# One graph attention layer on one core: the node stage reordered, a fourth gather buffer, marks made in the loop, x loaded by GpSimd

## The chip, the core and the metric

The kernel runs on one core of one Trainium2 chip. The metric is device time of one execution in microseconds, median of several runs. The core has five instruction streams: TensorE (PE), VectorE (DVE), ScalarE (ACT), GpSimd (POOL) and SyncE (SP, which here only issues DMAs). Each runs its own instructions in program order and waits for the others by semaphores.

## The reference

12,500 nodes with 128 channels, 400,000 edges sorted by their destination, 32 edge attributes, 8 heads of 16.

```python
h = relu(layernorm(x))
message = (h @ w_src + b_src)[src] + (h @ w_dst)[dst]
rad = silu(silu(edge_attr_32 @ w1 + b1) @ w2 + b2) @ w3 + b3
message = (message * edge_weight1 * rad) @ w_sep + b_sep      # 8 heads x (16 alpha + 16 value)
score = einsum('ehk,ahk->eh', smooth_leaky_relu(alpha), alpha_dot)
att = segment_softmax(score, dst)
out = x + segment_sum(value * att, dst) @ w_proj + b_proj
```

## The kernel before

**Tables.** `x` stands in 98 tiles of 128 nodes, taken four at a time as Q = 25 quads. For each quad, `stats` (DVE, L237) and `scales` (ACT square root L242, DVE L243 and L244) give mean and scale, `norm` (ACT L253, POOL L256, two tiles each) normalises, `turn` (PE L265, DVE L267) transposes and applies the ReLU, and `products(i, 0)` multiplies by w_src and `products(i, 1)` by w_dst (PE L276, ACT copy L282, SP stores L290 and L292 to the DRAM tables t_src and t_dst). The loop over i runs them ahead of each other by fixed distances. From i = 10 on, each round makes a product of both tables, the targets ten quads behind. Beside these stand the loads of weights and constants (`weights_list`, SP), and the order check: `falls` compares each destination with the next (DVE L309), `fits` counts the violations (PE L321 and L323, DVE to L326) into the number `bad`. `spans`, `cuts` and `places` prepare small tables; the end of `cuts` (L403 to L408) writes a DRAM row `same` which tells, edge by edge, whether a segment begins.

**Branch.** All engines then load `bad` (L1517). At zero the sorted-by-destination path `windows()` runs, the only one that these inputs take; `Else` is a general path that does not run.

**Main loop.** The edges form 782 sections of 512 (`SEC`), two to a step: `step(k)` for k = -5 to 390 (NP = 391 steps), software-pipelined by hand. For a step k:
- `gather(k, f)` (POOL L877, two calls a step, four gathers of 128 rows each): an indirect DMA brings rows t_src[src] into a tile `gs`. It goes out in step k - 2. `gs` has three buffers for each f, so a gather waits till the tile of step k - 3 was read.
- `load_w` (SP L849) brings 1024 edge weights to all partitions as w_b, three buffers; `load_d`, `load_md` (d_b, md), `load_e` (ACT L825, edge attributes e_t) the rest.
- `e_T`, `mlp1` to `mlp3` and `radial` (L887 to L936) make the radial weights, `sources` (PE L944) transposes the gathered rows, `one_hot_T` and md (L951) add the target rows, `message` (DVE L958) forms the message mT.
- `alphas` (PE L964, ACT L966, DVE L971) and `scores` (PE L980, ACT L992 or L997) make scores Sp, which SP stores to DRAM and reads back as S (L995, or L998 and L1003) in blocks of MP = 8 steps. A block's softmax follows: the flags sm of `load_sm` (L1006), spread over the partitions by PE (L1013), the running maxima (DVE L1018, L1023), the subtraction (L1032), the exponential Pr (ACT L1028) and its transposes (PE L1047, ACT L1050 and L1057).
- Twelve steps later (LAG), `values` (PE L1077, DVE L1079), `one_hot` and `sums` (PE L1090, DVE L1094) add values into a window of 64 nodes, ob, which is stored twice: to the accumulator agg (L1114) and, by `store_win` (L1098), to a table of window rows.

The zeroing of agg (L140, L142, SP) also runs in the first steps.

**Tail.** After the last gathers come steps NP to NP + 12, with the jobs listed at L1414 for the rows on window borders: `block_rows` (rr, L1164), `last_rows`, `block_totals` and two scatters comb into agg (POOL L1228, behind 11 others). Between these steps ACT loads x back, as x_fin (L1450, L1452). `final` divides, projects and adds x.

**What sets the order.** It is written out by hand: each engine's stream is the order in which `step` and the node stage's loop call the functions. A tile name with `bufs=n` turns over n buffers, and a new writer waits for the readers of the tile n turns back.

Of the kernel before, what the change touches and what calls it, by code (L numbers as in the profile page):

```python
# [30 lines left out]
P = 128  # L31
# [25 lines left out]
def gnn_kernel(ctx: ExitStack, tc: tile.TileContext, a: dict, out: bass.AP):  # L57
# [9 lines left out]
    NX = -(-NP // MP) * MP * PR  # L67
# [17 lines left out]
    same = dram.tile([1, NX + 1], BF16, name="same")  # L85
# [44 lines left out]
    nc.vector.scalar_tensor_tensor(spread, below, float(H), above, op0=ALU.is_lt, op1=ALU.mult)  # L130
    zc = 5
# [26 lines left out]
    with tc.tile_pool(name="node", bufs=2) as np_, tc.tile_pool(name="node1", bufs=1) as n1, \  # L158
# [32 lines left out]

        def load_targets():
# [16 lines left out]
        def weights_list():  # L209

            pairs = []
            for name, t in wt.items():
                ap = a[name]
# [13 lines left out]
            return [lambda t=t, ap=ap: nc.sync.dma_start(out=t, in_=ap) for t, ap in pairs]  # L227
# [31 lines left out]
        def turn(i):  # L259
# [3 lines left out]
            for t in range(t0, t1):  # L263
# [3 lines left out]
            nc.vector.tensor_scalar(x_all[:, t0:t1, :].rearrange("p u n -> p (u n)")[:, :w],  # L267
                                    pt.rearrange("p u n -> p (u n)")[:, :w], 0.0, None, op0=ALU.max)

        def products(i, k):  # L270
# [6 lines left out]
            u = 4 * (i % 2) if k else 0  # L277
            if u == 0:
                mds[k] = np_.tile([P, 4 + 4 * k, C], F32, name=f"ms{k}", bufs=4 if k else 6)
# [3 lines left out]
            if k and i % 2 == 0 and i + 1 < Q:  # L283
# [27 lines left out]
        def fits():  # L311
# [14 lines left out]
            nc.vector.tensor_copy(bad, sum_)  # L326
            nc.sync.dma_start(out=ends_d[:, 1:2 * NS + 1].rearrange("o (p c) -> (o p) c", p=NH),
# [8 lines left out]
            places_load()  # L336
# [15 lines left out]

        def places():

            on = n1.tile([NC, P], F32, name="on")
            nc.vector.tensor_tensor(on, to[:, 0, :], to[:, 1, :], op=ALU.is_equal)
            nc.vector.scalar_tensor_tensor(on, on, SKIP, to[:, 0, :], op0=ALU.mult, op1=ALU.add)
# [28 lines left out]
        def cuts():  # L386

            pv = nps.tile([P, 4, P], F32, name="pt")
            nc.tensor.matmul(pv[:, 0, :], bvb, w_proj, start=True, stop=True)
            nc.vector.tensor_add(b_out, pv[:, 0, :], b_out)  # L390
            nc.tensor.transpose(pv[:, 1, :], bvb, ident)
            nc.vector.tensor_scalar(bare[:, 0:C], pv[:, 1, :], -1e-16, None, op0=ALU.mult)
            nc.vector.tensor_copy(z.rearrange("p (t c) -> p t c", c=ROW),
                                  bare[:RP].unsqueeze(1).to_broadcast([RP, zc, ROW]))
# [1192 lines left out]
```

## Time and profile before

| what | us |
|---|---|
| median of 3 runs | 4141.16 (4141.04 to 4141.25) |
| profiled execution | 4142.2 |
| span from its first to its last instruction | 4140.4 |
| first gather starts | 77.37 |
| last gather ends | 4008.67 |
| POOL: gathers of L877 | 3125, busy 2971.4 |

The busy shares are of the span. In the group rows, a line holds the engine, the operation, the tiles by the program's names, the count, busy time and mean nanoseconds; behind the second bar stands the idle time of the engine just ahead, and what ended most of it. In rows in order of time, the start and the length come first, and the bracket gives the idle time ahead and what ended it; "issue" means that nothing was waited for. "SPq", "ACTq" and "POOLq" are issues of DMAs.

### The profile page before, as it was taken

The page shows a single profiled execution, that of the slowest core. Times are in us where ns is not written, and L with a number is a line of the kernel's source. Part 1 is how long each engine was busy: PE and PEld are TensorE (multiplying, and loading weights), DVE is VectorE, ACT ScalarE, POOL GpSimd, SP SyncE. Part 2 cuts the span into 40 slices and gives each one's busy share as a digit, 9 for nine tenths or more (in the row PEclk, how much of TensorE's full clock was granted, in tenths as well). Part 3 has the DMA queues.
Part 4 walks back from the last instruction along what each step waited for, and adds up shares of the span by engine and source line. Part 5 has one row for each costly group of instructions (what it writes and reads, how often), then busy time and mean ns, then how long its engine had stood idle before and what let it go on. Part 6 is the DMA issues. An engine that isn't in the chain of part 4 may idle for free. (4 is left out here: it accounts for less than half of the span.)

```text
span 4140.4 us, 87674 instructions
## 1 busy us (share of the span) xinstructions
PE 3922.6 (95%) x29351; PEld 2370.2 (57%) x29351; DVE 3079.2 (74%) x6182; ACT 1895.2 (46%) x4549; POOL 3031.8 (73%) x3218
## 2 busy tenths in 40 slices
PE   7789999999999999999999999999999999999997
PEld 6355555655555555555555555555555555555556
DVE  5567777777777778777777777777777777777775
ACT  5344444444444444444444444444444444444442
POOL 4777777777777777777777777777777777777762
PEclk8899999999999999999999999999999999999998
DMA  7767777767777777777777776767767767777754
GB/s 264 226 168 195 194 181 199 199 180 191 201 187 182 196 190 181 193 198 190 180 194 196 178 197 181 188 172 191 188 171 192 188 180 179 190 184 172 193 157 179
DMA packets 593219, 782.99 MB, mean 189 GB/s; under 512 B 125441, under 2 KB 392062, under 8 KB 592628
## 3 DMA queue, kind: packets, MB, share of 16 engines
q1 hardware_dynamic: 384520, 513.29, 42.8%
q0 software_dynamic: 100416, 205.44, 23.4%
q10 hardware_dynamic: 107820, 58.56, 5.0%
q8 instruction: 234, 3.83, 0.4%
q14 instruction: 229, 1.88, 0.1%
HBM read 637.82 MB, written 139.23 MB: 188 GB/s over the span
## 5 line engine op out<-in xcount | busy, mean ns | idle before, releaser
L877 POOL DMA_INDIRECT gs<-t_src,idx x3125 | 2971.4, 951 | 975.8 <-issue 792.2
L966 ACT ACTIVATE sl<-pa,c_b_a 128x512 f32<-128x512 f32 x782 | 536.9, 687 | 1117.4 <-PE pa L964 1106.3
L971 DVE SCALAR_TENSOR_TENSOR al<-pa,sl 128x512 f32<-128x512 f32 x782 | 539.4, 690 | 518.1 <-ACT sl L966 508.8
L1077 PEld LDWEIGHTS V<-c_w_v,mT 128*128 128x128 f32 x6064 | 737.7, 192 | 298.0 <-DVE ob L1094 156.0
L1077 PE MATMUL V<-c_w_v,mT 128*128 128x128 f32 x6064 | 867.7, 286 | 0.0
L964 PE MATMUL pa<-mT,c_w_a 128*128 128x512 f32 x1564 | 804.6, 596 | 3.8 <-DVE mT L958 2.5
L1079 DVE TENSOR_TENSOR pvx<-V,Pem 128x512 f32<-128x512 f32 x758 | 519.3, 685 | 236.9 <-PE V L1077 222.3
L944 PEld LDWEIGHTS pm<-ident,gs 128*128 128x128 f32 x3125 | 395.5, 141 | 516.4 <-issue 392.2
L936 DVE SCALAR_TENSOR_TENSOR rad<-p,c_fc_b,w_b 128x512 f32<-128x512 f32 x782 | 550.0, 745 | 121.6 <-PE p L928 90.4
L944 PE MATMUL pm<-ident,gs 128*128 128x128 f32 x3125 | 497.7, 276 | 75.1 <-DMA gs<-t_src,idx 73.8
L958 DVE SCALAR_TENSOR_TENSOR mT<-pm,c_b_src,rad 128x512 f32<-128x512 f32 x782 | 550.1, 745 | 5.2 <-PE pm L951 4.8
L1090 PEld LDWEIGHTS misc<-pvx,oh 128*64 128x64 f32 x6250 | 353.1, 138 | 316.2 <-ACT h L900 303.4
L914 ACT ACTIVATE h<-p,b 128x512 f32<-128x512 f32 x391 | 287.9, 736 | 405.4 <-PE p L911 317.9
L1090 PE MATMUL misc<-pvx,oh 128*64 128x136 f32 x6250 | 453.5, 287 | 19.8 <-ACT h L900 13.6
L928 PE MATMUL p<-h,w3b 64*128 64x512 f32 x1564 | 409.0, 600 | 7.7 <-ACT h L914 7.4
L951 PE MATMUL pm<-ohT,m 64*128 64x512 bf16 x2346 | 322.4, 380 | 0.0
L896 PE MATMUL m<-eT,w1b 64*128 64x256 f32 x782 | 277.3, 435 | 1.0 <-ACT eT L889 1.0
L896 PE MATMUL misc<-eT,w1b 64*128 64x256 f32 x782 | 277.3, 435 | 0.0
L997 ACT ACTIVATE Sp<-m,b_s 128x512 f32<-128x512 f32 x192 | 131.7, 686 | 301.0 <-PE m L980 299.0
L911 PE MATMUL p<-h,w2b 64*64 64x256 f32 x3128 | 260.6, 404 | 2.1 <-DVE rad L936 2.1
L900 ACT ACTIVATE h<-misc,b 128x256 f32<-128x256 f32 x391 | 192.8, 493 | 150.1 <-PE misc L896 148.4
L1063 DVE TENSOR_TENSOR oh<-lane,misc 128x504 f32<-128x504 f32 x391 | 261.3, 668 | 0.0
(174 smaller groups left out, 3685.4 us busy)
## 6 DMA issues: line engine op xcount, KB each, us to landing
w_b<-in_edge_weight SPq DMA_DIRECT2D x390, 512.0 KB
d_b<-in_dst SPq DMA_DIRECT2D x390, 256.0 KB
gs<-t_src,idx POOLq DMA_INDIRECT x3125
e_t<-in_edge_attr ACTq DMA_DIRECT2D x390, 128.0 KB
sc_d<-Sp SPq DMA_DIRECT2D x192, 256.0 KB
win<-ob SPq DMA_DIRECT2D x390, 68.0 KB
agg<-ob SPq DMA_DIRECT2D x782, 33.5 KB
md<-t_dst SPq DMA_DIRECT2D x782, 32.0 KB
```

The source lines that it names most:

```text
L877: nc.gpsimd.indirect_dma_start(out=gs[:, t, :], out_offset=None, in_=t_src[:, :], in_offset=bass.IndirectOffsetOnAxis(ap=idx[:, t0 + t:t0 ...
L896: nc.tensor.matmul(p1[q], w1b[s, :], eTs[k][s, :], start=True, stop=True)
L928: nc.tensor.matmul(p3s[k][:, f, 0:SEC], w3b[s, :], h2s[k][s, :], start=True, stop=True)
L936: nc.vector.scalar_tensor_tensor(rad[:, s], p3[:, f, 0:n], b3, w_g[k][:, s], op0=ALU.add, op1=ALU.mult)
L944: nc.tensor.matmul(pms[k, f][:, t * T:(t + 1) * T], gs[:, t, :], ident, start=(t == 0), stop=False, is_transpose=True, skip_group_check=True)
L958: nc.vector.scalar_tensor_tensor(mTs[k][:, s], pms.pop((k, f))[:, 0:n], b_n, rad[:, s], op0=ALU.add, op1=ALU.mult)
L964: nc.tensor.matmul(pa[:, 0:n], w_a, mTs[k][:, f * SEC:f * SEC + n], start=True, stop=True)
L966: nc.scalar.activation(sl[:, 0:n], pa[:, 0:n], AF.Silu, bias=b_a, scale=1.0)
L971: nc.vector.scalar_tensor_tensor(al, pa, 0.25, sl, op0=ALU.mult, op1=ALU.add)
L1077: nc.tensor.matmul(V[:, t, :], mTs[c][:, o:o + T], w_v, start=True, stop=True)
L1079: nc.vector.tensor_mul(pvx[c][:, f, 0:n, 0:C].rearrange("p t (h k) -> p t h k", h=H), V[:, 0:n, :].rearrange("p t (h k) -> p t h k", h=H), ...
L1090: nc.tensor.matmul(acc[f * W:(f + 1) * W, :], ohs[c][:, f * TS + t, :], pvx[c][:, f, t, :], start=(t == 0), stop=(t == n - 1), skip_group_ ...
```

## The change

In the node stage all 25 source products come ahead of the target products. The statistics run two quads further ahead, `h` has six buffers, ACT normalises one tile of a quad and POOL three, ACT applies the ReLU of odd quads, and the rows of t_src are stored two quads at a time. `falls` follow target products 0 to 3, and `count`, the part of `fits` that makes `bad`, target product 6. The smaller preparations move behind them. Five weights that only `Else` reads are loaded there, the other loads alternate between SP and ACT, and ACT runs one Silu ahead of the branch.

In the loop, `gs` has four buffers, `w_b` two and `ob` three; `load_w` goes out one step ahead rather than two, and d_b and w_b of step 0 ahead of the loop. `same` is no longer written: `load_sm` loads the destinations of a block and `marks` compares them on DVE two steps later, 49 times.

In the tail POOL loads x_fin behind its 11 scatters, and ACT stores the last rows rr straight from ob, step by step, where SP stored windows and read them back.

```diff
@@ norm, turn, products
-            hs[i] = np_.tile([P, 4, C], F32, name="h", bufs=4)
+            hs[i] = np_.tile([P, 4, C], F32, name="h", bufs=6)
...
-                if t - t0 < 4 - 2:
+                if t == t0:
...
+            if i % 2:
+                nc.scalar.activation(x_w, p_w, AF.Relu)
+            else:
+                nc.vector.tensor_scalar(x_w, p_w, 0.0, None, op0=ALU.max)
...
-                mds[k] = np_.tile([P, 4 + 4 * k, C], F32, name=f"ms{k}", bufs=4 if k else 6)
+                mds[k] = np_.tile([P, 8, C], F32, name=f"ms{k}", bufs=4)
@@ cuts: the flags
-            nc.scalar.dma_start(out=same[:, 0:E].rearrange("o (p c) -> (o p) c", p=P), in_=sm)
...
-            nc.scalar.dma_start(out=same[:, E:NX + 1], in_=more)
@@ loop of the node stage
-            if i >= 10:
-                products(i - 10, 1)
+            if i >= 25:
+                products(i - 25, 1)
             products(i, 0)
-            if i + 5 < Q:
-                stats(*quads[i + 5])
-            if i % 2 and i + 4 < Q:
-                scales(quads[i + 4][0], quads[min(i + 5, Q - 1)][1])
+            for j in range(i + 7 if i else 5, min(i + 8, Q)):
+                stats(*quads[j])
+            if i == 0:
+                scales(quads[5][0], quads[6][1])
+            if i % 2 and i + 6 < Q:
+                scales(quads[i + 6][0], quads[min(i + 7, Q - 1)][1])
...
             if i >= 3:
-                for load in (next(more, None), next(more, None)):
+                for eng in (nc.sync, nc.scalar):
+                    load = next(more, None)
                     if load:
-                        load()
-            if 8 <= i < 12:
-                falls(i - 8)
+                        load(eng)
             if i == 13:
                 fits()
-        for i in range(Q - 10, Q):
+        places_load()
+        for i in range(Q - 25, Q):
             products(i, 1)
-            if i == Q - 6:
+            if i < 4:
+                falls(i)
+            elif i == 6:
+                count()
+            if i == Q - 10:
                 spans()
-        cuts()
+                places_make()
+            elif i == Q - 6:
+                cuts()
+            elif i == Q - 4:
+                score_bias()
+            elif i == Q - 3:
+                places()
+        warm = n1.tile([1, 1], F32, name="warm")
+        nc.scalar.activation(warm, eps[0:1, :], AF.Silu)
@@ the loop's tiles
-                w_g[k] = lp.tile([P, PR], F32, name="w_b", bufs=3)
+                w_g[k] = lp.tile([P, PR], F32, name="w_b", bufs=2)
...
-                gs = lp.tile([P, TS, C], F32, name=f"gs{f}", bufs=3)
+                gs = lp.tile([P, TS, C], F32, name=f"gs{f}", bufs=4)
...
-                ob = sp.tile([P, ROW], F32, name="ob", bufs=5)
+                ob = sp.tile([P, ROW], F32, name="ob", bufs=3)
@@ load_sm and the new marks
-                at = same[0:1, m * MQ * SEC:m * MQ * SEC + 1]
-                nc.sync.dma_start(out=sms[m], in_=bass.AP(at.tensor, at.offset, [[SEC, MQ], [1, SEC + 1]]))
+                t = dms[m] = sp.tile([MQ, SEC + 2], I32, name="dm", bufs=1)
...
+                nc.sync.dma_start(out=t[q0:q1, :], in_=bass.AP(
+                    at.tensor, at.offset + e0 + q0 * SEC, [[SEC, q1 - q0], [1, SEC + 2]]))
+
+            def marks(m):
+                t = dms.pop(m)
+                sms[m] = sp.tile([MQ, SEC + 1], BF16, name="sm")
+                nc.vector.tensor_tensor(sms[m], t[:, 0:SEC + 1], t[:, 1:SEC + 2], op=ALU.not_equal)
@@ step
-                if has(k + 2):
-                    load_w(k + 2)
+                if has(k + 1) and k > -1:
+                    load_w(k + 1)
...
-                        if k == NP + LAG:
-                            last_rows_2()
+                        if c - 1 >= last * SB:
+                            last_rows(c - 1)
...
+                if has(k - 2) and (k - 2) % MP == 4:
+                    marks((k - 2) // MP)
@@ tail
-            x_loads = load_xb(x_fin)
+            load_xb(x_fin, nc.gpsimd)
...
+            def last_rows(c):
+                q, s = width(last) // 2, 2 * (c - last * SB)
...
                 for i in range(2):
+                    nc.scalar.dma_start(out=rrs[last][i * q + s:i * q + s + 2, :],
+                                        in_=accs[c][i * (W - 1):i * (W - 1) + W + 1:W, :])
...
-                for _ in range(3):
-                    next(x_loads, None)
```

What stands in the engines' streams, first on PE at the end of the node stage. `pt<-ident,h` are transposes of `turn`, `pm<-w_nodes,x_all` the products (four matmuls to a quad, source and target alike), `tot` the sums of the order check. Before:

```order
L265 MATMUL pt<-ident,h 128x128 x4
L276 MATMUL pm<-w_nodes,x_all 128x128 x8
L265 MATMUL pt<-ident,h 128x128
L265 MATMUL pt<-ident,h 128x84
L276 MATMUL pm<-w_nodes,x_all 128x128 x13
L276 MATMUL pm<-w_nodes,x_all 84x128
L276 MATMUL pm<-w_nodes,x_all 128x128 x37
L276 MATMUL pm<-w_nodes,x_all 84x128
```

After, from the same place on:

```order
L269 MATMUL pt<-ident,h 128x128
L269 MATMUL pt<-ident,h 128x84
L283 MATMUL pm<-w_nodes,x_all 128x128 x5
L283 MATMUL pm<-w_nodes,x_all 84x128
L283 MATMUL pm<-w_nodes,x_all 128x128 x28
L328 LDWEIGHTS ones_b
L328 MATMUL tot<-gt,ones_b 1x512
```

Before, each round held eight product matmuls, and ten target quads followed the last source quad (84x128 is its last tile). After, the sources end before any target; seven target quads (28 matmuls) stand between them and the check's sums, and 18 quads behind.

Second, ACT behind the last scores (Sp). Before:

```order
L992 ACTIVATE Sp<-m_51451,b_s 64x128
L992 ACTIVATE Sp<-m_51451,b_s 32x384
L1450 DMA x_fin<-xb 128x1792 x3
L1057 COPY pvx<-Pem 128x4x8 x2
L1450 DMA x_fin<-xb 128x1792 x3
L1057 COPY pvx<-Pem 128x4x8 x2
L1450 DMA x_fin<-xb 128x1664
L1452 DMA x_fin<-xb 84x128
L1057 COPY pvx<-Pem 128x4x8 x2
L1028 ACT_TABLE_LOAD
L1028 ACTIVATE Pr<-M 128x512
```

After:

```order
L1011 ACTIVATE Sp<-m_51522,b_s 64x128
L1011 ACTIVATE Sp<-m_51522,b_s 32x384
L1092 COPY pvx<-Pem 128x4x8 x6
L1063 ACT_TABLE_LOAD
L1063 ACTIVATE Pr<-M 128x512
L1085 COPY Pem<-misc 128x256 x2
```

The eight loads of x_fin are gone from between the copies. They are on POOL, whose stream after the change reads there:

```order
L896 DMA gs_51217<-t_src,idx 128x128
L1263 DMA agg<-e_t,ids 12500x136 x11
L1481 DMA x_fin<-xb 128x1792 x6
L1481 DMA x_fin<-xb 128x1664
L1482 DMA x_fin<-xb 84x128
L1263 DMA agg<-comb,ids 12500x136 x2
```

They stand between the 11 early scatters and the two of comb.

More of the change, by code (lines that the diff above doesn't have):

```diff
@@ L776, in windows @@
             prep, e_g, d_g, w_g, md, gath = {}, {}, {}, {}, {}, {}
[L777 to L778 removed]
+            eTs, h1s, h2s, ohT, m3, mr, mTs, als, S_all, sms, Ps, Pem, pvx, ohs, accs, xs, Ms, pms, p3s, rads, rel, locs, made, dms = (
+                {} for _ in range(24))
             def prep_load(u):
@@ L1520, in gnn_kernel @@
     with fit.Else():
+        for name in spare:
+            nc.sync.dma_start(out=wt[name], in_=a[name])
         for i in range(NZ):
```

79 lines of the change are left out of this document (37 added, 42 removed).

## Prediction, made before the changed kernel ran

> **What bounds the kernel now.** I read the page's busy shares and costliest groups first, then busy time by stretches, then the order of time of each engine at the start, at the one long stall, and behind the last gather. The profiled execution took 4142.2 us around a span of 4140.4; the runs' median is 4141.16. I work every term out in the span and take the sum off the median, 1.0 us below the profiled execution.
>
> ```profile
> span 4140.4 us, 87674 instructions
> PE 3922.6 (95%) x29351; PEld 2370.2 (57%) x29351; DVE 3079.2 (74%) x6182; ACT 1895.2 (46%) x4549; POOL 3031.8 (73%) x3218
> L877 POOL DMA_INDIRECT gs<-t_src,idx x3125 | 2971.4, 951 | 975.8 <-issue 792.2
> 2000.00:2200.00 200.00, 193.91 (x1459) 115.39 (x1458) 152.36 (x308) 91.23 (x220) 151.49 (x160) 1.00 0.74 194
> ```
>
> The shares mislead: PE shows 95% and POOL 73%, but POOL's gap between gathers is mostly "issue", which means that it waited for nothing. In 200 us it issues 160 gathers, 1.25 us each (0.95 busy, 0.30 issue), and never more. PE is busy 193.9 of the same 200 us. So POOL paces the middle and PE follows 3% behind its limit. The gathers form one chain from the first to the last:
>
> ```profile
> 77.37 1.19 POOL L877 DMA_INDIRECT gs<-t_src,idx  x1 [15.91 <-DMA t_dst<-ms]
> 225.54 0.94 POOL L877 DMA_INDIRECT gs<-t_src,idx  x1 [7.07 <-PE pm L944]
> 4007.73 0.94 POOL L877 DMA_INDIRECT gs<-t_src,idx  x1 [0.30 <-PE pm L944]
> ```
>
> The span is 77.4 us ahead of the first gather, 3931.3 from it to the end of the last (4008.67), and 131.7 behind it. Inside the chain is one long stop, 7.07 us, 6.8 more than the usual 0.30. The number of gathers and their work stay, so the change can gain ahead of the chain, at that stop, and behind the chain.
>
> **Head: the node stage.** Ahead of 77.37 POOL idles 15.9 us for node rows. The program's waits say for which: all t_src stores (the row's name, t_dst, is the nearest landing), and `bad`, which was made long before.
>
> ```profile
> 46.40 0.14 DVE L326 CAST bad<-sum__607 1x1 int32<-1x1 f32 x1
> 72.87 0.85 SPq L292 DMA_DIRECT2D t_src<-ms  x1
> 15.74 2.08 PE L276 MATMUL pm<-w_nodes,x_all 128*128 128x128 f32 x8
> 63.86 1.95 PE L276 MATMUL pm<-w_nodes,x_all 128*128 128x128 f32 x16
> 65.83 11.80 PE L276 MATMUL pm<-w_nodes,x_all 128*128 128x128 f32 x104
> 61.28 1.04 ACT L282 COPY ms<-pm 128x512 f32<-128x512 f32 x2
> 60.50 0.88 ACT L253 ACTIVATE h<-x_all,shift,rstd 128x128 f32<-128x128 f32 x2 [0.54 <-DVE shift L244]
> ```
>
> The last t_src store is issued at 72.87 and the gather starts 3.65 us behind that issue. From quad 10 on every step carries a source and a target product: PE takes 16 matmuls and 4 transposes for 2.2 us, so 15 quads carry 0.9 us each (11.80/13, a quad being 8 of the 104 records) of target work ahead of the last source. The change takes these 15 x 0.9 = 13.5 us out of the way. What is late next is ACT: a quad has a copy of 0.52 (1.04/2), one norm of 0.44 (0.88/2; there were two) and half a ReLU, taken as half a copy, 0.26, together 1.22; I add 0.23 for what is left of the 0.54 wait and the small operations, 1.45. While the weights load (12 quads, 3 to 14) ACT issues one DMA more in each, 0.48 (1.45/3 in the e_t row below): 1.93. Product 2 comes at about 16.7 (second half of the 15.74 row), then 12 x 1.93 and 10 x 1.45 give 54 for the last source product. Its store lands near 60 if SP, with 13 t_src stores where there were 25, keeps up.
>
> Now `bad` comes from behind seven target products: 7 x 0.9 = 6.3, so 60.3; then what it took before, from the first row sum on PE (43.26) to the cast (46.40 + 0.14), 3.3, then load and branch, an estimate of 1 to 2: 65 to 66. So `bad` replaces the stores as what ends last. I take 66, range 62 to 70: **-11 us** (-7 to -15). Nothing waits behind the gather on POOL but gathers.
>
> ```profile
> 43.26 1.48 PE L321 MATMUL tot<-gt,ones_b 128*1 128x512 bf16 x7
> ```
>
> **The stop at 225 us.** The gather there is number 112 of the chain, the first of step 14, and with three buffers it waits for PE's transposes of step 11's rows, the line named in its row. PE was late since it waited 21.5 us for the scan that reads the first block's scores S, which SP stored and reloaded late:
>
> ```profile
> 218.62 0.69 PE L887 MATMUL m<-ident,e_t 128*128 128x128 f32 x2 [21.53 <-DVE M L1018]
> 217.34 1.22 DVE L1018 TENSOR_TENSOR_SCAN M<-m,S 128x512 f32<-128x512 f32 x1 [20.28 <-DMA S<-sc_d]
> 204.71 0.35 SPq L998 DMA_DIRECT2D sc_d<-Sp  x1
> 213.40 0.57 SPq L1003 DMA_DIRECT2D S<-sc_d  x1
> ```
>
> With a fourth buffer step 15 waits for step 11: eight gathers, 8 x 1.25 = 10.0 us of room. But the head has moved the chain 11 us up, and PE's chain must follow. Its start, however, hangs on t_dst, finished when PE's products are (the same work in all), so near 80 as now. What it gains are these waits:
>
> ```profile
> 83.56 6.96 SPq L856 DMA_DIRECT2D md<-t_dst  x4
> 86.14 0.37 ACTq L405 DMA_DIRECT2D same<-sm  x1
> 86.34 1.23 DVE L407 MEMSET more<- 1x1409 bf16 x1 [0.23 <-DVE sm L404]
> 89.13 1.45 ACTq L825 DMA_DIRECT2D e_t<-in_edge_attr  x3
> 91.56 0.66 PE L887 MATMUL m<-ident,e_t 128*128 128x128 f32 x2 [10.79 <-DMA e_t<-in_edge_attr]
> ```
>
> ACT's first e_t load stood behind the `same` stores, whose flags DVE made until 87.6; without them it goes at about 81, 8 us earlier; SP loses the wait in md. With e for the time by which the S chain moves up, the gathers gain min(11 + 6.8, 10 + e). I take e = 7.5 (2 to 11): **-17 us** for head and stop together (-10 to -21).
>
> **Tail.** ACT's x_fin loads stand ahead of the copies and the exponential that PE waits for:
>
> ```profile
> 4025.42 7.31 ACTq L1450 DMA_DIRECT2D x_fin<-xb  x3
> 4025.59 4.02 SPq L995 DMA_DIRECT2D S<-Sp  x6
> 4033.04 2.19 PE L1090 MATMUL misc<-pvx,oh 128*64 128x136 f32 x16 [3.48 <-ACT pvx L1057]
> 4039.66 0.69 DVE L1032 TENSOR_TENSOR M<-S,M 128x512 f32<-128x512 f32 x1
> 4045.35 0.34 ACT L1057 COPY pvx<-Pem 128x32 f32<-128x32 f32 x2 [10.39 <-DMA x_fin<-xb]
> 4047.00 0.63 ACT L1028 ACTIVATE Pr<-M 128x512 f32<-128x512 f32 x1
> 4047.68 0.69 PE L1047 MATMUL misc<-ident,Pr 128*128 128x128 f32 x2 [4.27 <-ACT Pr L1028]
> ```
>
> With ACT free, PE's 3.48 goes and M is ready at 36.9 instead of 40.35; Pr follows at once, PE comes to its transposes at 47.68 - 4.27 - 3.48 = 39.9 and finds it there: -7.75. Next late could be the landing of S<-Sp, whose issues end at 4029.61, 7.3 us ahead of M's new time; between them lie the landing, two scans (1.22 each, the L1018 row) and the subtraction (0.69), so a landing over 4 us would take some of it back; I allow for 3. The loads go behind POOL's scatters:
>
> ```profile
> 4075.20 0.97 POOL L1228 DMA_INDIRECT agg<-comb,ids  x1 [52.42 <-ACT pvx L1057]
> 4083.13 0.71 SPq L1405 DMA_DIRECT2D rr<-win  x2
> 4084.73 1.77 SPq L1114 DMA_DIRECT2D agg<-ob  x2
> 4087.02 0.26 ACT L1219 COPY comb<-misc 28x136 f32<-28x136 f32 x1 [1.57 <-PE misc L1218]
> 4088.48 0.91 POOL L1228 DMA_INDIRECT agg<-comb,ids  x1 [12.32 <-DMA agg<-ob]
> ```
>
> POOL's 52.4 idle us cover them: eight issues at a gather's 1.25 are 10. If that cover were gone, the scatter would be up to 10 us late. At the very end SP's last agg store no longer stands behind the rr<-win reload, so the scatter follows comb (4087.28) instead of 4088.48: -1. Tail: **-8.75** (-3 to -11).
>
> **What should cost nothing.** A w_b load is issued a step later, with two buffers. For the last step the load and its use are both the last rows of their kind:
>
> ```profile
> 3994.71 0.34 SPq L849 DMA_DIRECT2D w_b<-in_edge_weight  x1
> 4012.64 1.01 DVE L936 SCALAR_TENSOR_TENSOR rad<-p,c_fc_b,w_b 128x512 f32<-128x512 f32 x2
> ```
>
> They lie 17.9 us apart; a step of eight gathers (10.0) leaves 7.9 for 512 KB, which at the 194 GB/s of the row above take 2.7. Bounds: 0 and, if it lands late, the price of the fourth rival. The 49 marks are DVE work: a 128x512 two-input operation takes 0.69 (L1032 above), so 34 us of DVE in all, on an engine busy 152 of 200; cover: its idle quarter; without it, at most 34. Beside the gathers their cost is bounded by all that the present DVE work costs them: the mean of 951 ns in the group against a normal 944 is 7 x 3125 = 22 us, for 49 more of some 6000 operations under 1 us:
>
> ```profile
> L877 POOL DMA_INDIRECT gs<-t_src,idx x3125: 938/944/1435, 77.4 to 4007.7; - x196
> L1032 DVE TENSOR_TENSOR M<-S,M x49: 691/692/741, 223.6 to 4039.7; 128x512 f32<-128x512 f32 x49
> ```
>
> [...]
>
> ob with three buffers, rr with two, and the queue change of weights cost nothing that I can find: the first are free long before reuse (a step is 10 us, a store's landing a few), and the second moves an issue of about 0.45 us from SP to ACT, counted above.
>
> **Sum:** -17 - 8.75 = -25.75, and 4141.16 - 25.75 = **4115.4**.
>
> **The rivals.**
> 1. *The S chain stays where it is* (e = 0): SP's chain is held by the zero stores and DMA traffic, not by the start. For it: SP issues S<-sc_d 8.7 us behind the store of it (rows above), and the zero stores stand in SP's stream as before. Gathers gain 10 at most: 4141.2 - 10 - 8.75 = 4122.4. Chance 0.17.
> 2. *The tail keeps its length*: the last softmax is held by S or by POOL's x loads. Against it: M was ready 5.3 us ahead of ACT's table load. Then 4141.2 - 17 - 1 = 4123. Chance 0.12.
> 3. *`bad` takes the whole place of t_src*: seven target products and the sums come no earlier than 77, because ACT and POOL pace the sources at 2.2 us. Then the fourth buffer alone takes out the stop: 4141.2 - 6.8 - 8.75 = 4125.6. Chance 0.11.
> 4. *Slower: w_b becomes late.* If it lands more than 7.9 us behind its issue, rad, then PE, waits each step, and with PE at 97% of POOL's pace the wait goes into the step. Break-even is 25.75/391 = 0.07 us a step; 0.3 us would be +117, so 4141.2 - 25.75 + 117 = 4233. Against it: 2.7 against 7.9. Chance 0.04.
> 5. *The marks lock the gathers out* for their full length (the mechanism bounded at 34 us): 4141.2 - 25.75 + 34 = 4149, within 0.2%. Chance 0.03.
>
> **How the numbers follow.** The forecast has 0.53. 0.2%, about what a measurement of this kernel can tell from no change, is 8.3 us. The forecast with all its terms at their best ends is 4141.2 - 21 - 11 = 4109; with them at their worst, -10 - 3 = 4128. Rivals 1 to 3 lie inside. I widen the lower end to 4106 for the start's pace, which I reckon from groups, and set 4106 to 4130. Faster than 4132.9 are the forecast and rivals 1 to 3, 0.93; same, rival 5, 0.03; slower, rival 4, 0.04.
>
> **What would show it.** First gather at 62 to 70 with `bad` the last wait ahead of it; no stop over 2 us near 215; gathers still 1.25 us; no x_fin row in ACT's stream, Pr 28 to 31 us behind the end of the last gather (now 38.3), and the piece behind the last gather 123 instead of 131.7. It would be wrong if that piece stays at 131, if the first gather stays at 77, or if rad waits for w_b in the steady stretch.

## The result, and the profile after

The changed kernel takes 4144.97 us (median of 12 runs, 4137.45 to 4149.96), the kernel before in the same comparison 4141.1 (12 runs, 4139.89 to 4144.95). The ratio is 1.0007, with a 95% interval of 0.9998 to 1.0016: no difference that can be measured. 4115.4 was forecast, with a range of 4106 to 4130, so the prediction is wrong. The profiled execution of the changed kernel took 4148.57 us around a span of 4146.8.

First the page's span and the group of the gathers, which now carry the line L896:

```profile
span 4146.8 us, 87989 instructions
PE 3914.9 (94%) x29351; PEld 2369.2 (57%) x29351; DVE 3097.9 (75%) x6213; ACT 1896.6 (46%) x4537; POOL 3051.4 (74%) x3251
L896 POOL DMA_INDIRECT gs<-t_src,idx x3125 | 2978.7, 953 | 979.7 <-issue 774.5 <-DMA gs<-t_src,idx 48.3 <-PE pm L963 48.3
```

and the same 200 us of the steady stretch in the table by stretches (length; busy time and count of PE, PEld, DVE, ACT, POOL; clock, DMA share, GB/s):

```profile
2000.00:2200.00 200.00, 194.21 (x1454) 115.54 (x1453) 153.42 (x309) 91.32 (x220) 151.53 (x160) 0.99 0.72 192
```

Still 160 gathers in 200 us: the pace of the middle is what it was. POOL's stream in order of time, at the first gather, at the stop, and at the last gather:

```profile
60.66 1.67 POOL L896 DMA_INDIRECT gs<-t_src,idx  x1 [15.22 <-DVE base L386]
224.04 0.97 POOL L896 DMA_INDIRECT gs<-t_src,idx  x1 [8.96 <-PE pm L963]
4002.92 0.94 POOL L896 DMA_INDIRECT gs<-t_src,idx  x1 [0.30 <-issue]
```

The last gather ends at 4003.86. So the span divides anew:

| piece | before | after | change | forecast |
|---|---|---|---|---|
| ahead of the first gather | 77.37 | 60.66 | -16.7 | -11 |
| first gather to end of last | 3931.3 | 3943.2 | +11.9 | -6 |
| behind the last gather | 131.7 | 142.9 | +11.2 | -8.75 |
| span | 4140.4 | 4146.8 | +6.4 | -25.75 |

(-6 is the -17 of head and stop together, less the -11 of the head. "Head" is what lies ahead of the first gather, "chain" the gathers with the idle time between them, "tail" what lies behind the last one.) The head gave more than was forecast; the chain and the tail took it all back.

**Head.** In order of time, SP's last store of t_src, DVE's `bad`, and ahead of both the last run of products on PE:

```profile
48.71 7.79 PE L283 MATMUL pm<-w_nodes,x_all 128*128 128x128 f32 x68
51.34 0.76 SPq L299 DMA_DIRECT2D t_src<-ms  x1
58.70 0.14 DVE L333 CAST bad<-sum__823 1x1 int32<-1x1 f32 x1
```

`bad` is made 1.8 us ahead of the gather and 7 behind the issue of the last store of t_src, as the prediction had it. (The gather's row names `base`, the copy that follows `bad` on DVE; what POOL's load ahead of the branch waits for in the program is `bad`.) All of it is some 5 us earlier than reckoned, because the source products were through near 49 and not at 54.

**Chain.** The 11.9 are the stop (8.96 where it was 7.07, +1.9), four smaller stops between 100 and 160 us that were not there before (0.63 to 1.58 idle each, together 3.5 above the usual 0.30; before, two others had made 0.9), and the gathers' own length: 2978.7 - 2971.4 = +7.3.

The length of a stop doesn't say what the head and the fourth buffer gained together, since the chain now comes to it earlier. The start of one and the same gather does: the one behind the new stop, number 120 (counted from 0). It starts at 224.04 (the second row above), and before the change it started here:

```profile
235.85 0.94 POOL L877 DMA_INDIRECT gs<-t_src,idx  x1 [0.30 <-PE misc L896]
```

That is a gain of 11.8 where 17 was forecast. From its start to the end of the last gather it is 3779.8 us, before 3772.8: 7.0 more, where nothing was forecast.

**Tail.** Behind the last gather, SP's stream in order of time:

```profile
3986.89 0.39 SPq L1413 DMA_DIRECT2D e_t<-obs_d  x1
...
3990.88 0.33 SPq L1149 DMA_DIRECT2D agg<-ob  x1
4009.10 0.40 SPq L1413 DMA_DIRECT2D e_t<-obs_d  x1
4012.12 0.33 SPq L868 DMA_DIRECT2D w_b<-in_edge_weight  x1
...
4041.02 4.09 SPq L1014 DMA_DIRECT2D S<-Sp  x6
4045.16 0.63 SPq L1191 DMA_DIRECT2D mx<-max_d  x1
```

SP issues nothing from 3991.2 to 4009.1. The list of waits names the reason:

```profile
SPq L1149 <- DMA agg<-ob: 18.7, 8, 5.3
SPq L1413 <- DMA agg<-e_t,ids: 17.8, 1, 17.8
```

L1413 loads the window rows which POOL's 11 scatters add to agg, in four pieces, into buffers of e_t. The fourth waits 17.8 us for scatters (agg<-e_t,ids) of the first piece, since it has got the first piece's buffer. Behind it on SP stands the last w_b load, issued at 4012.12; before, it went at 3994.71. The rest follows, on DVE, PE and ACT:

```profile
4016.26 1.01 DVE L955 SCALAR_TENSOR_TENSOR rad<-p,c_fc_b,w_b 128x512 f32<-128x512 f32 x2 [8.99 <-DMA w_b<-in_edge_weight]
4047.60 0.48 DVE L1212 TENSOR_TENSOR_SCAN up<-cuts,up,mx 128x128 f32<-128x128 bf16 x1 [13.10 <-DMA mx<-max_d]
4050.71 0.58 PE L1048 MATMUL m<-sm,spread 16*128 16x512 bf16 x1 [14.04 <-DVE M L1053]
4053.32 0.63 ACT L1063 ACTIVATE Pr<-M 128x512 f32<-128x512 f32 x1 [19.39 <-DVE M L1067]
```

Pr starts 49.5 us behind the end of the last gather (before 38.3, forecast 28 to 31). A second wait stands in these rows: DVE's scan `up` waits 13.1 us for mx, a small table whose load SP issues only at 4045.16, behind the last scores' reloads and 18.7 us of waits for agg<-ob.

The wait at L1413 can be read in the program, without a run. The fourth load, before and after:

```
L1374 DMA e_t<-obs_d 128x2x136 [waits DMAHW5_49,PE_49]
L1413 DMA e_t<-obs_d 128x2x136 [waits DMASW7_49,DMAHW3_49,DMASW6_49,DMASW5_49]
```

Before, its buffer had last held edge attributes, read by PE. Now it is the first piece's, with three of POOL's DMAs (DMASW) to wait for. Nothing in the diff touches e_t. In the description of the kernel before it says that a new writer waits for the readers of the tile n turns back; here it doesn't hold: with four buffers the fourth load has the buffer of three turns back, that of the first piece, and before it had another. So the buffers don't simply turn round. That they are handed out as they come free in the program, and that the new order of other steps changed this, fits both programs and was not tried apart.

### The profile page after: what moved, and what is told of

Its sections match the earlier page's. It is cut to its first block, busy times and chain, and to the rows that moved or that the text cites. A ratio compares the mean times of both kernels' runs of the same rounds, so it can differ in the third digit from the quotient of the medians.

```text
span 4146.8 us, 87989 instructions
## 1 busy us (share of the span) xinstructions
PE 3914.9 (94%) x29351; PEld 2369.2 (57%) x29351; DVE 3097.9 (75%) x6213; ACT 1896.6 (46%) x4537; POOL 3051.4 (74%) x3251
## 5 line engine op out<-in xcount | busy, mean ns | idle before, releaser
L896 POOL DMA_INDIRECT gs<-t_src,idx x3125 | 2978.7, 953 | 979.7 <-issue 774.5
L1125 PE MATMUL misc<-pvx,oh 128*64 128x136 f32 x6250 | 455.1, 288 | 13.9 <-ACT h L919 11.2
```

The lines of the kernel that those rows point to most:

```text
L896: nc.gpsimd.indirect_dma_start(out=gs[:, t, :], out_offset=None, in_=t_src[:, :], in_offset=bass.IndirectOffsetOnAxis(ap=idx[:, t0 + t:t0 ...
L1125: nc.tensor.matmul(acc[f * W:(f + 1) * W, :], ohs[c][:, f * TS + t, :], pvx[c][:, f, t, :], start=(t == 0), stop=(t == n - 1), skip_group_ ...
```

## The experiments

The theories, by the letters that the expectations use:
- **A**: the tail is longer because of the fourth e_t load; a fifth e_t buffer takes that wait away.
- **B**: w_b with two buffers makes the first steps late, and so S and the stop.
- **C**: the marks, with two inputs in SBUF, lengthen the gathers beside them.
- **D**: POOL issues the x loads all at once, and that traffic delays the last softmax.
- **E**: the zero stores in SP's stream keep the score store, and so S, late.

Chips differ here: on those of e1 to e9 and e15 to e18 the kernel before took 5157 to 5193 us, and PE set the pace there. The page's busy shares and the list of waits of the changed kernel on one of them (e18) show it:

```profile
PE 4185.4 (81%) x29351; PEld 2479.2 (48%) x29351; DVE 3096.4 (60%) x6213; ACT 1893.8 (37%) x4537; POOL 3056.1 (59%) x3251
```
```profile
PEld misc L1125 <- issue: 617.6, 242, 5.1
PE misc L1125 <- issue: 421.0, 234, 4.3
```

PE is idle a fifth of the time, more than half of it in stretches in which it waits for nothing that the profile shows, up to 5 us long. The gathers then wait for PE, and a total says nothing of POOL's chain. So e1 to e9 left A, B and C open. Only e10 to e14 ran where POOL sets the pace, e10 on one chip and e11 to e14 on another.

### e1 to e9: buffers and marks, where PE sets the pace

e1 and e5 (A):

```diff
-                e_g[k] = lp.tile([T, 2, TS * RAD], F32, name="e_t", bufs=4)
+                e_g[k] = lp.tile([T, 2, TS * RAD], F32, name="e_t", bufs=5)
```

with the same edit at L1412. e2 and e6 (B); M gives up a buffer for the room:

```diff
-                w_g[k] = lp.tile([P, PR], F32, name="w_b", bufs=2)
+                w_g[k] = lp.tile([P, PR], F32, name="w_b", bufs=3)
...
-                Ms[m] = sp.tile([P, 2, SEC], F32, name="M")
+                Ms[m] = sp.tile([P, 2, SEC], F32, name="M", bufs=1)
...
-                if has(k + 1) and k > -1:
-                    load_w(k + 1)
+                if has(k + 2) and k > -2:
+                    load_w(k + 2)
```

e3, e7 and e9 have both edits. e4 and e8 (C) make the flags with one input in SBUF, by comparing the destinations with 0, so that they no longer tell where a segment begins:

```diff
-                nc.vector.tensor_tensor(sms[m], t[:, 0:SEC + 1], t[:, 1:SEC + 2], op=ALU.not_equal)
+                nc.vector.tensor_scalar(sms[m], t[:, 0:SEC + 1], 0.0, None, op0=ALU.not_equal)
```

> The changed kernel with five buffers for e_t instead of four, nothing else. Theory A: the tail grew because the fourth load of early rows (e_t<-obs_d) got the buffer of the first, so SP waited 17.8 us for POOL's scatters, with the last w_b and the S loads queued behind. Then that wait is gone, rad waits under 1 us for the last w_b, the piece behind the last gather falls from 142.9 to between 123 and 132, and the time from 4145 to between 4125 and 4134. Rival: the tail grew because x_fin, loaded by POOL, crowds the S loads and agg stores; then the wait goes but the piece stays over 139 and the time over 4141.

> The changed kernel with three w_b buffers and the load two steps ahead, as before (the scans' M gets one buffer instead of two to make room). Theory B: two w_b buffers slowed the start, 43 us of rad's waits, and that kept the S chain late; then these waits fall under 10 us, S<-sc_d is issued by 206 instead of 213, the stop at gather 120 falls from 9.0 to under 3, and the time by 6 to 9, to 4136 to 4139. Rival: the zero stores in SP's stream set the S chain; then the waits go but S<-sc_d stays within 2 us of 213, the stop stays at 8 to 10, and the time within 2 of 4145.

> Fifth e_t buffer and three w_b buffers together, M one. If A and B both hold: 4145 - 14 - 7, 4119 to 4128. If only A holds: 4127 to 4134. If neither: over 4140.

> The changed kernel, the marks' comparison of two shifted views replaced by a comparison of one view with zero, same 16x513 shape: leaves out the right flags, so segments come out wrong. Theory C: a Vector operation with two SBUF inputs makes the gather beside it longer (26 of 49 marks lie on a long gather, 0.33 us each); then the mean gather falls from 953 to 951 ns and the chain by 6 to 8 us. Rival: any work on DVE at that place does it; then the mean stays at 953 and the time within 2 of 4145.

| run | us | ratio to before | 95% |
|---|---|---|---|
| e1 | 5199.49 | 1.0010 | 0.9994 to 1.0027 |
| e2 | 5199.12 | 1.0015 | 1.0001 to 1.0029 |
| e3 | 5195.77 | 1.0001 | 0.9987 to 1.0015 |
| e4 | 5195.28 | 1.0005 | 0.9995 to 1.0015 |
| e5 | 5162.56 | 1.0015 | 0.9989 to 1.0041 |
| e6 | 5163.77 | 1.0009 | 0.9990 to 1.0029 |
| e7 | 5165.89 | 1.0016 | 0.9997 to 1.0035 |
| e8 | 5159.74 | 1.0001 | 0.9984 to 1.0018 |
| e9 | 5197.45 | 1.0007 | 0.9988 to 1.0025 |

The expected gains are not there, but that hits none of the theories. For A the wait itself is missing on such a chip: in e18, the changed kernel, the fourth e_t load is issued 4.7 us behind the third (22.2 in the profile above).

### e10: five e_t buffers, where POOL sets the pace

The edit of e1.

> The changed kernel with five e_t buffers, once more. Where the kernel before takes about 4141: theory A (e_t's fourth early-row load waited for POOL's scatters, with SP's last w_b and S loads behind): rad waits under 1 us for the last w_b, the piece behind the last gather 123 to 132 instead of 142.9, time 4125 to 4134. Rival (x_fin on POOL crowds SP): piece over 139, time over 4141.

4142.49 us against 4149.92 of the kernel before on the same chip: 0.9985 (0.9973 to 0.9996). The span is 4135.9, the last gather ends at 4002.97, and the tail is 132.9 us, 10.0 shorter than in the changed kernel's profile, and just over the 123 to 132 that was expected; the time is outside the expected 4125 to 4134. SP's stream in order of time:

```profile
3990.93 0.40 SPq L1413 DMA_DIRECT2D e_t<-obs_d  x1
3993.93 0.33 SPq L868 DMA_DIRECT2D w_b<-in_edge_weight  x1
...
4018.11 4.13 SPq L1014 DMA_DIRECT2D S<-Sp  x6
4022.29 0.62 SPq L1191 DMA_DIRECT2D mx<-max_d  x1
4024.18 13.72 SPq L1149 DMA_DIRECT2D agg<-ob  x2
```

The fourth load goes without a wait and the last w_b load ahead of the last gather's end. A is shown. Its size can also be read on one chip: e14 below, which still has four e_t buffers, has the same wait (its fourth load goes out 22.0 us behind the third) and a tail of 143.6; e11 on that chip, with five, has 135.4 (the two differ in w_b and the marks too). So it is worth some 8 to 10 us. But the tail stays 10 us over the forecast 123. What holds it now stands on POOL, DVE and ACT:

```profile
4019.80 3.76 POOL L1481 DMA_DIRECT2D x_fin<-xb  x7 [2.25 <-PE pm L1112]
4033.11 0.49 DVE L1212 TENSOR_TENSOR_SCAN up<-cuts,up,mx 128x128 f32<-128x128 bf16 x1 [9.51 <-DMA mx<-max_d]
4038.11 0.69 DVE L1067 TENSOR_TENSOR M<-S,M 128x512 f32<-128x512 f32 x1
4038.83 0.63 ACT L1063 ACTIVATE Pr<-M 128x512 f32<-128x512 f32 x1 [15.81 <-DVE M L1067]
```

POOL issues seven x loads in 3.8 us and an eighth behind them; the mx load goes out 2.5 us after the first, behind five of them, and its reader starts 10.8 us after its issue (before: 3.67, issued at 4030.17 and read at 4033.84). The subtraction for Pr stands behind this scan on DVE. That is theory D.

### e11: both edits

> Five e_t buffers and three w_b buffers, M one, where the kernel before takes about 4145: the fifth e_t buffer gave a piece behind the last gather of 132.9. Theory B (two w_b buffers slowed the start and kept S late): rad's waits at the start under 10 us, S<-sc_d by 202 instead of 206 to 213, no stop over 2 us near gather 120, time 4 to 9 below the version with five e_t buffers alone (whose profile is 4136 in span). Rival (zero stores in SP's stream set the S chain): waits go, S and the stop stay, time the same as with e_t alone.

4143.79 against 4147.83: 0.9988 (0.9978 to 0.9997), no better than e10. The reload of S says what B is worth. SP's issue of it in the changed kernel, in e10, in e11, and in e14, which has two w_b buffers and ran on e11's chip:

```profile
213.23 0.57 SPq L1022 DMA_DIRECT2D S<-sc_d  x1
```
```profile
206.43 0.57 SPq L1022 DMA_DIRECT2D S<-sc_d  x1
```
```profile
207.49 0.57 SPq L1022 DMA_DIRECT2D S<-sc_d  x1
```
```profile
207.55 0.57 SPq L1022 DMA_DIRECT2D S<-sc_d  x1
```

With three w_b buffers the eleventh pair of rad starts at 189.9, in e14 at 198.8 and in e10 at 197.5; S is reloaded within 1.1 us of the same time. B falls: the rad waits are there (43.0 us on DVE between 80 and 230 in the changed kernel, 0.9 in e11) and S does not hang on them.

These rows show something else: in e10, e11 and e14, and in e12 (207.04), S comes 5.7 to 6.8 us earlier than in the changed kernel's own profile. Gather number 120 starts at 218.3, 219.2, 219.6 and 218.5 in e10, e11, e12 and e14, which is 16 to 18 us ahead of the kernel before (235.85, and 236.34 in e13 on the chip of e11 to e14, whose chain is still that of the kernel before). The repairs tried don't account for it: e10's is a fifth e_t buffer alone, e14's the form of the marks alone. So the 11.8 of the first profile is not what the change always gives, and why S was late there is open.

### e12: the x loads behind Pr

e11, with the loads held back on POOL until Pr is made:

```diff
-            load_xb(x_fin, nc.gpsimd)
...
+                if j == 3:
+                    held_x = tail_pool.tile([1, 1], F32, name="held_x")
+                    nc.gpsimd.tensor_copy(held_x, Ps[LAST_M][0:1, 0:1])
+                    load_xb(x_fin, nc.gpsimd)
```

> As the run beside it with both repairs, and POOL's x_fin loads held back until Pr of the last block stands (a one-element copy of Pr on POOL ahead of them). Theory D (x_fin's 6.4 MB, loaded by POOL at once, slow SP's agg stores and the loads of mx and S behind them, 12.3 us on one store): M and Pr come 4 to 9 us earlier, the piece behind the last gather falls from 133 to between 122 and 129, time by 4 to 10 against the run beside it. Rival (M is late for SP's own order, whatever x does): that piece stays within 2 of the run beside it.

4143.74 against 4147.83, 0.9990 (0.9980 to 0.9999). The scan and Pr, and then the scan of the second, smaller mx, with SP's stream between them:

```profile
4023.57 0.49 DVE L1212 TENSOR_TENSOR_SCAN up<-cuts,up,mx 128x128 f32<-128x128 bf16 x1 [1.41 <-DMA mx<-max_d]
4029.11 0.63 ACT L1063 ACTIVATE Pr<-M 128x512 f32<-128x512 f32 x1 [7.52 <-DVE M L1067]
4030.47 3.75 POOL L1484 DMA_DIRECT2D x_fin<-xb  x7 [0.33 <-issue]
4032.31 8.34 SPq L1149 DMA_DIRECT2D agg<-ob  x2
4047.01 5.86 SPq L1149 DMA_DIRECT2D agg<-ob  x2
4055.09 0.28 DVE L1212 TENSOR_TENSOR_SCAN up<-cuts,up,mx 128x28 f32<-128x28 bf16 x1 [13.76 <-DMA mx<-max_d]
```

Pr comes 28.5 us behind the last gather, 8.4 earlier than in e11, within the forecast's 28 to 31. And the tail is 135.4 in both, where 122 to 129 was expected: the burst now meets SP's agg stores, which wait for each other (8.34 us for the first two), the second mx load goes out behind them at 4052.96, and the scan waits 13.8 for it. D is borne out in its first half, up to Pr. What the tail would be with no burst in its way was not measured where POOL sets the pace, so that the rest of it is the burst's doing is argued.

### e13: the kernel before, with x loaded by POOL

One part of the change alone.

```diff
-            x_loads = load_xb(x_fin)
+            for _ in load_xb(x_fin, nc.gpsimd):
+                pass
...
-                for _ in range(3):
-                    next(x_loads, None)
...
-            nc.scalar.dma_start(out=x_fin[:, t0:t1, :], in_=xb_v[:, t0:t1, :])
+            eng.dma_start(out=x_fin[:, t0:t1, :], in_=xb_v[:, t0:t1, :])
```

> The kernel before with one part alone: x_fin loaded by POOL behind its scatters instead of by ACT between steps. The prediction's term: the piece behind the last gather falls from 131.7 by 7.75, to 124. Theory D (the loads, all at once, slow SP's stores and loads): it falls by 0 to 3, or grows.

4149.71 against 4147.83, 1.0002 (0.9992 to 1.0012). By the tail term this edit should have been worth -7.75; the time's change lies between -3.3 and +5.0 by the interval, so that is excluded. Its tail is 137.8 in this one execution, 6.1 longer than in the profile before, which is from another chip. A stretch of 20 us in the table by stretches (last three columns: granted clock, DMA share, GB/s), before and in e13:

```profile
4030.00:4050.00 20.00, 11.77 (x63) 8.74 (x64) 8.62 (x17) 3.73 (x11) 0.00 (x0) 0.64 0.79 284
```
```profile
4030.00:4050.00 20.00, 7.90 (x71) 6.45 (x70) 7.93 (x17) 1.90 (x6) 4.33 (x8) 0.75 0.88 332
```

and e13's rows in order of time, on SP and DVE:

```profile
4035.18 0.62 SPq L1156 DMA_DIRECT2D mx<-max_d  x1
4037.03 13.04 SPq L1114 DMA_DIRECT2D agg<-ob  x2
4045.48 0.48 DVE L1177 TENSOR_TENSOR_SCAN up<-cuts,up,mx 128x128 f32<-128x128 bf16 x1 [11.16 <-DMA mx<-max_d]
```

The same load that was read 3.67 us after its issue is read after 10.3. Before, ACT's queue had let out the eight loads over 20 us:

```profile
4033.04 1.55 ACTq L1450 DMA_DIRECT2D x_fin<-xb  x3
4044.20 0.33 ACTq L1450 DMA_DIRECT2D x_fin<-xb  x1
```

Ahead of these rows stand the first three (4025.42, 7.31 us long, the third at 4032.40), so two large loads were out when SP issued mx at 4030.17. In e13 POOL issues all eight from 4031.31 to 4035.64, and mx, at 4035.18, comes behind them. It was not ACT's work that spread them: in the table's 20 us ACT is busy for 3.7, and its queue pauses twice, for 6 us ahead of the third load and over 9 ahead of the seventh, with its copies waiting behind. That the burst delays mx is shown with the rest of the kernel unchanged; what it costs the whole kernel is less than the spread of the runs can tell.

### e14: marks with one input, where POOL sets the pace

The edit of e4.

> The changed kernel with marks of one SBUF input, which leaves out the right flags. Theory C (two SBUF inputs make the gather beside them longer): mean gather 951 instead of 953 to 955, gathers' chain 6 to 8 us shorter than the changed kernel's 3943, time 4137 to 4139 where the kernel before takes 4141. Rival (any DVE work there does it): mean stays, time within 2 of the changed kernel's.

4147.39 against 4147.83, 0.9998 (0.9988 to 1.0008). The marks are this group in the changed kernel (minimum, median and maximum in ns):

```profile
L1044 DVE TENSOR_TENSOR sm<-dm x49: 673/675/731, 165.4 to 4018.1; 16x513 bf16<-16x513 int32 x49
```

From the trace I summed what the gathers from 300 us on took over the usual 944 ns: 27.2 us in the changed kernel, 19.5 before. Of 57 gathers that overlap a mark, 26 are over 0.98 us, with 8.5 us of excess; with one input it is 18 of 53, with 2.2 (other operations of DVE ran beside some of them too). In e11 and e12, with two inputs on e14's chip, the excess is 10.9 and 9.8. So the marks' form matters, as C has it. That it is the second input alone is not shown: the operation with one input is another one and shorter, 411 ns where it was 675, though by its length alone some 5 us would be left and not 2.2. The total doesn't tell: the mean gather stays at 953 ns, since the usual one takes 947 ns in this execution and 944 in the changed kernel's, which over 3125 gathers is 9 us by itself. The expected 4137 to 4139 was missed.

### e15 to e18: x spread out, zero stores on ACT

e15 (D) issues one x load a step on POOL, each behind a step's ob, and has five e_t buffers; e16 (E) puts the zero stores on ACT's queue, with five e_t buffers:

```diff
+                if j < 8:
+                    nc.gpsimd.tensor_copy(held_x, accs[k - LAG - 1][0:1, 0:1])
+                    next(x_loads, None)
```
```diff
-        nc.sync.dma_start(out=av[:, i * zc * ROW:(i + 1) * zc * ROW], in_=z)
+        nc.scalar.dma_start(out=av[:, i * zc * ROW:(i + 1) * zc * ROW], in_=z)
```

e17 has both, and e18 is the changed kernel itself again, beside them.

> The changed kernel with five e_t buffers, and POOL's eight x_fin loads spread over the first eight steps of the tail (ahead of each, POOL copies one element of that step's ob). Theory D (the loads all at once fill the DMA engines for some 20 us, and mx and the agg stores stand behind them): the scan of up waits under 4 us for mx instead of 9 to 14, the piece behind the last gather falls from 133 to between 120 and 127, time 6 to 13 below the version with five e_t buffers alone. Rival (SP's own order keeps mx late): the piece stays over 130.

> The changed kernel with five e_t buffers, and the zero stores of agg issued by ACT instead of SP. Theory E (SP's waits at the zero stores keep the sc_d store and the S load late): S<-sc_d is issued by 198 instead of 206 to 213, the stop at gather 120 falls from 4.7 to 9 to under 2, time 4 to 8 below the version with five e_t buffers alone. Rival (DMA traffic or the scores themselves set it): S moves by less than 4 us, the stop stays over 3, or ACT, blocked at the stores, makes it later.

> Five e_t buffers, x_fin spread, zero stores on ACT. If D and E hold: 10 to 20 below the version with five e_t buffers alone, 0.4% to 0.7% below the kernel before. If D alone: 6 to 13 below it.

> The changed kernel as it is, for a second profile and for its time beside the three others. Expected: 1.0007 of the kernel before as at first (0.999 to 1.002), the fourth early-row load waiting for POOL's scatters, a piece of 140 to 146 behind the last gather; S<-sc_d between 206 and 213, which tells how far that varies between executions.

Against 5156.52 of the kernel before: e15 5163.42, 1.0022 (0.9996 to 1.0047); e16 5159.35, 1.0002 (0.9981 to 1.0023); e17 5161.07, 1.0013 (0.9989 to 1.0037); e18 5155.85, 1.0006 (0.9986 to 1.0026). PE sets the pace here, so the totals don't tell. e18's profile missed the rest of what was expected of it too: S was reloaded at 251.15 and the tail was 162.8.

The traces say something of E. From SP's last store of the first block's scores to their reload (sc_d<-Sp to S<-sc_d) are 8.66 us in e18, with the zero stores in SP's queue (9.55 in e15, 8.76 in the changed kernel, 8.69 before), and 4.79 in e16, with them on ACT's (4.40 in e17). So the zero stores hold the scores up by about 4 us, a part of what E says. Whether it is the shared queue is not told apart: the last zero store went out 2.3 us ahead of that store of scores in e18, and 8.6 and 5.1 ahead in e16 and e17. What it would be worth to the stop where POOL sets the pace wasn't measured.

Of D they tell little. The scan `up` waits 12.0 and 12.9 us for mx over both its places in e15 and e17, and 9.2 in e16, where the loads go at once; but most of that passes ahead of mx's issue by SP. From issue to reader it is 2.8 and 2.7 us for the first mx load of e15 and e17, and 3.4 in e16, whose burst had gone out 14 us earlier. The spread loads' tails are 167.3 and 167.0, e16's 162.2: no gain here.

## Why the prediction was wrong

1. **Bound: right.** 160 gathers in 200 us before and after, and the three pieces of the span add up to the result.
2. **Head: right in mechanism, too small in size.** `bad` ends the wait, as said; -16.7 where -11 stood. The mis-sized term is the pace of the sources: 12 quads at 1.93 and 10 at 1.45 were reckoned. On PE, of fourteen quads in a row, the first and the last start so:

```profile
29.64 1.16 PE L283 MATMUL pm<-w_nodes,x_all 128*128 128x128 f32 x8
47.63 1.06 PE L283 MATMUL pm<-w_nodes,x_all 128*128 128x128 f32 x8
```

   That is 17.99/13 = 1.38 us a quad. For "load and branch, an estimate of 1 to 2" no row before the change had a number; here it is 1.8 us from the end of the cast to the gather.
3. **The stop: wrong in the changed kernel's profile, with e.** "I take e = 7.5" is the step that failed there: S was reloaded at 213.23 where it had been at 213.40, so e = 0, and rival 1 is what happened: gather number 120 gained 11.8 us, not 17. PE did begin 12.8 us earlier (78.74 against 91.56), and lost it again in the steps up to 225. One part is shown: w_b, loaded a step later, made rad wait 43.0 us in the first eleven steps, the mechanism of rival 4 in a place where I hadn't looked for it. But e11 against e14 shows that S doesn't hang on that. In e10, e11, e12 and e14 S came 5.8 to 7.0 us ahead of 213.40, nearly the e that was forecast, and number 120 started 16 to 18 us earlier: there the term came out. So e differs between executions, and what makes S late in some is open. (The prediction's own formula gives -17.5 for e = 7.5 and -12 for e = 2, where it has -17 and -10.)

   **Behind the stop: left out.** From number 120 on, the chain took 7.0 us more, and the forecast had nothing for it. In e14 that stretch is 4.0 longer than in e13, in e11 and e12 5.6 and 4.4. The marks are one part (point 7); e14, in which they cost 2 us, shows that they are not all of it.
4. **Tail: wrong, and the largest miss.** -8.75 forecast, +11.2 measured, 20 us apart. Two steps failed. "What should cost nothing" left out that a tile's buffer can change hands when other steps move: that wait is worth some 8 to 10 us (e10, and e11 against e14). And "the loads go behind POOL's scatters ... POOL's 52.4 idle us cover them" priced the loads by POOL's time only. What they cost is the way of other transfers: this edit alone gave no gain in the place of -7.75 (e13), and a tail that was 6.1 longer in its profile. (e10's tail, 132.9, is 4.9 shorter than e13's; what of the other edits gave that wasn't measured apart, but for the 1.2 of point 5.) Rival 2 had the right place and a time of 4123; its mechanism was right in naming POOL's loads, and its size was too small since it let the tail keep its length. The forecast's own chain was sound as far as Pr: with mx on time, Pr stands at 28.5 (e12). That what Pr gains reaches the end was the next step to fail: e12's tail is no shorter than e11's. The list of what could be late next had the landing of S, and mx was not on it.
5. **The very end: right.** -1 was forecast for SP's last store. From DVE's last ob (4090.20, before 4082.08) to the scatter it is now 5.2 us, before 6.4.
6. **w_b, 17.9 us of room against 2.7 needed: right in the steady stretch.** Of the nine waits of rad for w_b (52.0 us), eight lie ahead of 230 us and one, 9.0, in the tail; none lies between. At both ends, where PE runs behind or SP is held, the sum of 17.9 - 10 doesn't apply.
7. **Marks: not free.** Beside them the gathers lost 8.5 us, 0.17 us for each of 49 marks of 0.675, a quarter of the full lock that rival 5 priced at 34. That all present excess together is 22 us was a correct bound on the size and no reason to put nothing. The Trainium skill (SBUF — State Buffer, section SBUF: two separate sides) states that a Vector operation with two SBUF inputs contends with a GpSimd operation that reads SBUF, and that the second to start waits until the first is done; of DMAs that GpSimd issues it reports a probe that `tensor_tensor` did not stall, and infers why. These gathers did get longer beside the marks, and less so with one input (8.5 against 2.2, e14), but it was no full wait: only 26 of 57 that overlapped a mark were longer at all, by 0.33 us each.
8. **Chances.** Faster had 0.93. Every rival that was faster shared the tail's -8.75 or the stop's -6.8 with the forecast, so they were not independent of it, and "the same" was left to the marks alone.

The best version that was run is the changed kernel with five e_t buffers (e10): 0.9985 (0.9973 to 0.9996) of the kernel before; e11 and e12 can't be told apart from it.

## What to carry to other kernels

Read the waits of the changed program wherever a ring of buffers is shared, also for tiles that the diff does not name: reordering other steps can hand a buffer to another reader, and one load that waits 18 us holds all that its queue has behind it. Loads that one engine's queue lets out over a long time can arrive as one burst from an idle engine; the price is then what small transfers on other queues wait, not the issuing engine's time. Room given to one chain is worth only what the chain that it then waits for allows, and that chain has to be followed to its own first wait. Where two changes move the same stretch, compare the start of one and the same operation before and after, not the length of a stop, and take a second profile before a term is called right or wrong.

## What was not expected of the hardware

- A small load (mx, 64 KB) was read 3.67 us after its issue with two of the large x loads issued ahead of it, and 10.3 and 10.8 us after it with eight and five of them, sent by POOL within 4.4 us (e13, e10). In the 20 us of the table the 16 DMA engines were 0.88 busy at 332 GB/s in e13, where they had been 0.79 at 284.
- The same program takes about 4145 or about 5156 us depending on the chip, with POOL or PE as the bound; the granted clock of the slower profile was 0.949 over the span, of the faster 0.985, and much of PE's idle time there, 617.6 us ahead of the weight loads of one line alone, has no releaser in the trace.
- The usual length of a gather was 944 or 947 ns from one execution to the next, which is 9 us of the span, as much as the effect of the marks.
